# Two-layer masked attention on 16 graphs: other steps for four pieces of batch 14's work, two counts in halves, another buffer and an earlier inversion at the end

## The chip, the cores and the metric

The kernel runs on one core of a Trainium2 chip. The metric is the device time of one execution in microseconds (us); lower is better. The kernel before was run three times: 3083.88 us in the median, from 3083.51 to 3085.02.

## What is computed

The reference takes `x` (16 x 1024 x 256, float32) and a 0/1 adjacency `adj` (16 x 1024 x 1024, int32) and applies two layers of attention with a residual. Cut to what matters:

```python
h = jnp.maximum(_layernorm(x), 0.0)
x = x + L0(h, adj)      # 4 heads of 64
h = jnp.maximum(_layernorm(x), 0.0)
x = x + L1(h, adj)      # 8 heads of 32, with biases on q, k, v
...
# in a layer, for each batch and head:
scores = where(adj > 0, q @ k.T / sqrt(D), -inf)
out = concat_heads(softmax(scores) @ v) @ Wo.T + bo
```

All of it is float32. The softmax is computed as exp(score) over the sum of the exps, without a maximum; a test at the end (`chk`) tells whether a sum left its bounds.

## The kernel before, in words

**Batches and layers.** There are 16 batches (b = 0 to 15). The list of work is layer 0 of batch b + 1, then layer 1 of batch b, and so on, so layer 0 of one batch stands beside layer 1 of another. The last 32 steps are layer 1 of batch 15 alone.

**Groups and steps.** A layer of a batch is cut into two halves of 512 queries (`qh`) and two groups of heads (`g`), so four groups, written (qh, g). A group of layer 1 has 8 steps of 128 keys (j = 0 to 7). For a step i of layer 1, TensorE (PE) makes the scores of four heads (L539, eight matmul instructions into two PSUM pairs), VectorE (DVE) applies the mask and moves them to SBUF (L562, two instructions, one for each pair), and ScalarE (ACT) takes the exp (L568, two instructions). Two steps later (`LEAD`) PE multiplies the exps with v (`weigh`, L580). After an odd step GpSimd (POOL) adds that step's two tiles `p` onto those of the even step before it (L695, two instructions). Tiles of odd steps live in two buffers, so DVE can write step i + 4 only when POOL has added step i. Tiles of even steps live in seven buffers (tag `p0`), so step i + 14 takes the buffer of step i.

**Sums.** The added tiles of a group are added again in memory by a DMA that POOL issues (L681, `accumulate`, 1 MB each). Then `count` (L425) has PE multiply the result with ones, into the PSUM tile `pz`; `halves` does the same in two calls of 256 columns at two steps. From `pz` comes the reciprocal of the sums in five moves, each with its own step: `spread` (L445 copies `pz` on ACT, L458 sends it through four small DMAs into 128 lanes), `invert` (L466 on DVE, then L468, a DMA to DRAM called `vd`), `fetch` (L477, four DMAs that spread `vd` over the partitions as `inv`), `normalize` (L485 on POOL, one multiplication of `cat` for each group of heads), and, for the second group of a half, `end_half`: the product with Wo on PE (L521, sixteen matmuls, the tile `py`) and its addition to x on DVE (L526). The last group of all (`hurry`) uses `finish` instead: it takes the reciprocal on DVE straight from PSUM (L505), multiplies (L506), makes the product in quarters (L496), adds it (L511) and sends it out (L514).

**Units.** The inputs of a layer are made half by half: `stats` (L198 and L199 on DVE for each of four tiles of 256 columns, then four small operations on POOL, L209 to L212, for all four tiles at once), `norm` (L221 on ACT, one for each tile), `turn_blocks` (L273 on DVE), `put_blocks` (L278) and `place_blocks` (L285), which go through DRAM, then the units `k`, `q`, `values` on PE (L307, L383), each emptied by ACT or DVE. `add_bias` is L230 on POOL.

**Order.** The order is written out by hand. `later(i, f)` hangs a piece of work on step i; steps are numbered through. At a step the program issues the scores, then `weigh` of two steps before and the POOL additions, then the counts due, then mask and exp, then the other work due in the order in which it was hung up, and last the units named in `LARGE` (k, q, values, end_half). At an even step with such a unit, `weigh` is put off to the next step. Each engine takes its instructions strictly in this order, and so do the DMA queues of SP and POOL.

**Names used below.** `c` is the first step of layer 1 of batch 14 (`second[14]`, step 704); c + 5 is five steps later. At these steps layer 1 of batch 14 runs, the inputs of layer 1 of batch 15 are made, and the last half of layer 0 of batch 15 is finished: its last group ends at step c - 1 and its `end_group` counts from c + 1. In the diff, `gr.inp.b == B - 1` with layer 0 is this half, `gr.inp.b == B - 2` is layer 1 of batch 14, and `gr.pairs` is layer 1 of batch 15. The groups (0,0), (0,1), (1,0) of batch 14 call `end_group` at c + 9, c + 17 and c + 25. Group (1,0) of batch 15 calls it at step 761; the last scores are those of step 767.

Of the kernel before, what the change touches and what calls it, by code (L numbers as in the profile page):

```python
# [10 lines left out]
F32 = mybir.dt.float32  # L11
# [7 lines left out]
P = 128  # L19
# [71 lines left out]
def fast_program(ctx, tc, a, w, loads, chk):  # L91
# [5 lines left out]
    B, N, E = x.shape  # L97
# [6 lines left out]
    work = ctx.enter_context(tc.tile_pool(name="work", bufs=2))  # L104
# [11 lines left out]
    def psum_pair(name):  # L116
        return ps_s.tile([P, 2, 512], F32, tag="ps_s", name=name)
# [12 lines left out]
    def tiled(cols):  # L130

        return cols.rearrange("p (t g q) -> p t g q", g=4, q=32)
# [260 lines left out]
    class Group:  # L393
# [93 lines left out]
        def finish(self):  # L487

            inp, qh = self.inp, self.qh
            inv = work.tile([P, 512], F32, tag="inv", name=f"inv_{self.n}")  # L490
            py = psum_pair(f"py_{self.n}").rearrange("p a (t e) -> p (a t) e", e=E)
            rows, cat = xs[inp.b, qh], self.half.cat
            dst = quarters(out, inp.b, qh)

            def product(i, c):
                nc.tensor.matmul(  # L496
                    py[:, i, :], cat[:, c, ts(i, P)], w.o[self.layer][:, c, :],
                    start=c == 0 and i % 2 == 0, stop=c == 1 and i % 2 == 1,
                )

            for i in range(4):
                product(i, 0)
            for h in range(2):
                q = ts(h, 256)
                nc.vector.reciprocal(tiled(inv)[:, ts(h, 2)], by_tile(self.s)[:, ts(h, 2)])  # L505
                nc.vector.tensor_mul(cat[:, self.g, q], cat[:, self.g, q], inv[:, q])  # L506
                for i in (2 * h, 2 * h + 1):
                    product(i, 1)
            for h in range(2):
                t = ts(h, 2)  # L510
                nc.vector.tensor_add(rows[:, t, :], py[:, t, :], rows[:, t, :])  # L511
                for g in range(4):
                    queue = nc.scalar if g % 2 else nc.sync
                    queue.dma_start(dst[g][:, t, :], rows[ts(g, 32), t, :])  # L514
# [91 lines left out]
    class Stream:  # L606
# [12 lines left out]
        def later(self, i, f, *args):  # L619
            self.due.setdefault(i, []).append((f, args))  # L620
# [62 lines left out]
        def count_steps(self, i, st):  # L683


            gr, j = st.gr, st.j
            if gr.hurry and j >= NT - 2:
                if st.last:
                    self.counted(i, gr)
                gr.count([of[:, r, :] for of in st.halves for r in range(2)], False, st.last)  # L690
            elif j % 2:
                one = self.steps[i - LEAD - 1].p
                for k, of in enumerate(st.halves):
                    half = one[:, ts(k, 2), :]
                    nc.gpsimd.tensor_add(half, half, of)  # L695
                if gr.pairs and (st.last or gr.hurry):
                    self.later(i + 2, gr.count, one, j == 1, st.last)
                elif gr.pairs:
                    self.halves(i + 3, gr, one, j == 1, False)
                elif j == 1:  # L700
                    gr.one = one
                elif gr.brief:
                    if j == 3:
                        self.accumulate(one, gr.one)
                        self.later(i + 6, gr.count, one, True, False)
                    elif j == 5:
                        self.halves(i + 5, gr, one, False, False)
                    else:
                        self.later(i + 4, gr.count, one, False, True)
                elif j == 5:  # L710
                    gr.two = one
                elif st.last and gr.qh and not gr.g:
                    self.accumulate(one, gr.two)
                    for k, of in enumerate((gr.one, one)):
                        self.later(i + gr.waits, gr.count, of, not k, k == 1)
                elif st.last and gr.last:
                    self.accumulate(gr.two, gr.one)
                    self.later(i + 1, self.accumulate, one, gr.two)
                    self.later(i + gr.waits, gr.count, one, True, True)
                elif st.last:  # L720
                    self.accumulate(gr.two, gr.one)
                    self.later(i + 2, self.accumulate, one, gr.two)
                    if gr.g:
                        self.halves(i + gr.waits, gr, one, True, True)
                    else:
                        self.later(i + gr.waits, gr.count, one, True, True)
                else:
                    self.accumulate(one, gr.one)
                    gr.one = one
# [12 lines left out]
        def end_group(self, i, gr):  # L742

            if gr.hurry:
                for f in (gr.spread, gr.finish, gr.inp.test):
                    self.later(i, f)
                return

            if gr.layer == 0:
                if gr.g == 0:  # L750
                    gr.half.first = gr
                    return
                early = gr.inp.b == 0 and gr.qh
                self.later(i + (2 if early else 3), gr.count_added)
                at = (3, 4, 5, 7, 13) if gr.qh else (3, 5, 6, 7, 11)
                if gr.inp.b == B - 1 and gr.qh:
                    at = 3, 6, 7, 9, 13
                if gr.inp.b == 0:
                    at = (2, 3, 4, 5, 8) if gr.qh else (3, 5, 6, 7, 9)
            else:  # L760
                at = ((9, 11, 13, 19), (8, 12, 14, 17, 19), (7, 9, 11, 14), None)[2 * gr.qh + gr.g]
                if gr.pairs:
                    at = 2, 5, 6, 7, 9
                elif gr.last:
                    at = 4, 6, 7, 9, 11
            for k, f in zip(at, (gr.spread, gr.invert, gr.fetch, gr.normalize)):
                self.later(i + k, f)
            if gr.last:

                k = 7 if gr.layer or gr.inp.b == 0 else 25 if gr.inp.b == B - 1 else 37  # L770
                self.later(i + k, gr.inp.test)
            if gr.g == 1:
                self.later(i + at[4], gr.end_half)
# [80 lines left out]
    later = stream.later  # L854

    def norms(inp, half, *at, whole=False, bias=None):

        for k, i in enumerate(at):
            f, rest = (inp.norm, (whole,)) if k > 1 else (inp.stats, ())
            later(i, f, half, (2, 3) if k % 2 else (0, 1), *rest)  # L860
        later(at[3] + 1 if bias is None else bias, inp.add_bias, half)
# [6 lines left out]
    def block_inputs(inp, half, turn, put, place, *at):  # L868

        later(turn, inp.turn_blocks, half)  # L870
        later(put, inp.put_blocks, half)
        later(place, inp.place_blocks, half)
        parts = inp.k_part, inp.q_part, inp.values_part
        for i, f, part in zip(at, (inp.k, inp.q, inp.values), parts):
            if type(i) is tuple:
                for m in range(2):
                    later(i[m], part, half, m)
            else:
                later(i, f, half)
# [9 lines left out]
    for t in range(NT):  # L889
        i = 7 + 2 * t  # L890
# [8 lines left out]
    for b in range(B - 1):  # L899
        mine, a, c = inputs[1][b], first[b + 1], second[b]  # L900
        if b == 0:

            norms(mine, 0, a + 4, a + 6, a + 7, a + 8, whole=True)
            half_inputs(mine, 0, a + 10, a + 12, a + 13, a + 14)
            norms(mine, 1, a + 10, a + 11, a + 12, a + 13, whole=True)
            half_inputs(mine, 1, a + 15, c, c + 6, c + 2)
        else:
            norms(mine, 0, a - 27, a - 26, a - 19, a - 17, bias=a)
            block_inputs(mine, 0, a - 14, a - 11, a - 5, a, a + 2, a + 8)
            norms(mine, 1, a - 14, a - 14, a - 8, a - 6, bias=a + 6)  # L910
            block_inputs(mine, 1, a, a + 6, a + 7, c, c + (6 if b + 2 < B else 10), c + 2)
        for i, u in zip((0, 2, 4, 6, 7, 9, 11, 13), range(NT)):
            later(a + i, masks[b].second, u)
        if b + 2 < B:
# [13 lines left out]
            at = 5, 8, 10, 12, 14, 45, 49, 51, 53  # L928
# [3 lines left out]
                later(a + at[t + 1] + (1 if t == 4 else 2), mask.flip, t)  # L932
        else:
            last, e = inputs[1][b + 1], c + 32
            later(c + 5, last.stats, 0)
            later(c + 10, last.norm, 0)
            later(c + 13, last.add_bias, 0)
            block_inputs(last, 0, c + 11, c + 12, c + 13, c + 18, c + 22, c + 26)
            later(c + 18, last.stats, 1)
            later(c + 22, last.norm, 1)  # L940
            later(c + 23, last.add_bias, 1)
# [252 lines left out]
```

## Time and profile before

| what | value |
| --- | --- |
| median of three runs | 3083.88 us |
| time of the profiled execution | 3083.88 us |
| its span, first to last instruction | 3082.1 us |
| PE busy | 3061.3 us, 99% of the span |
| DVE, ACT, POOL busy | 80%, 73%, 80% |
| share of PE on the chain that ended last | 92% |
| scores of step c | at 2847.24 us |
| scores of step c + 5 | at 2869.97 us |
| unit k of step c + 18 | at 2913.32 us |
| unit k of step c + 32 | at 2958.86 us |
| scores of the last step (767) | at 3058.69 us |

The page is read from the span down: it gives busy time for each engine, then groups of instructions by line. Since PE is busy nearly everywhere, a mean says little. The timeline of a stretch, which gives the start, the length, the engine, the line and in brackets the idle time before the instruction with what ended it, says where PE took longer than its work needs. Times from here on are us from the start of the span.

### The profile page before, as it was taken

To read this page: it belongs to the slowest core of one execution; us is meant where nothing else is said; L and a number is where in the kernel's file an instruction comes from. 1 tells how busy PE (TensorE), PEld (TensorE's weight loads), DVE (VectorE), ACT (ScalarE), POOL (GpSimd) and SP (SyncE) were. 2 spreads that over 40 slices of the span, in tenths; PEclk is the share of its full clock that TensorE was granted. 3 is DMA by queue.
4 is the path that set the end of the run, shared out by engine and by line. 5 is a ranking of instruction groups with operands and counts; after the bars stand their busy time and mean duration, and the time that the engine had idled before them with its cause. 6 is when DMAs were issued, how large, how long until landed. Compare 5 with 4: busy or idle time off the path is not lost.

```text
span 3082.1 us, 46012 instructions
## 1 busy us (share of the span) xinstructions
PE 3061.3 (99%) x16678; PEld 1199.8 (39%) x16678; DVE 2464.4 (80%) x2712; ACT 2242.9 (73%) x2478; POOL 2462.1 (80%) x1584
## 2 busy tenths in 40 slices
PE   9999999999999999999999999999999999999998
PEld 4443433434334343343433334343343433434333
DVE  6778787887878878787887878878788787887877
ACT  5668777777777767777777777777777777776775
POOL 3578788787887878878788887888878778787886
PEclk9999999999999999999999999999999999999999
DMA  4226556464563645546456463654636546463431
GB/s 134 63 61 147 129 123 135 121 141 121 129 145 110 139 130 133 136 110 138 124 129 138 120 139 108 147 123 122 141 104 144 132 122 138 118 143 86 100 82 34
DMA packets 263548, 372.77 MB, mean 121 GB/s; under 512 B 58768, under 2 KB 218768, under 8 KB 242448
## 3 DMA queue, kind: packets, MB, share of 16 engines
q0 software_dynamic: 23472, 170.93, 28.2%
q1 hardware_dynamic: 239520, 198.56, 22.2%
q8 instruction: 133, 2.18, 0.3%
q14 instruction: 103, 0.84, 0.1%
q10 hardware_dynamic: 320, 0.26, 0.0%
HBM read 149.95 MB, written 47.96 MB: 64 GB/s over the span
## 4 chain that ended last, share of the span: by engine, by line
PE 92%; DVE 2%; DMA 2%; POOL 1%; issue 1%; SPq 1%; ACT 1%; DVEq 0%; ACTq 0%; POOLq 0%
PE ps L539 31%; PE po L580 28%; PE pq L307 10%; PE py L521 7%; PE pv L383 6%; PE pq L348 5%; PE pz L425 4%; PE pv L367 2%; DVE p L562 1%; DMA p<-p 1%; POOL p L695 1%; DMA sums<-s 0%; DMA inv<-vd 0%; ACT p L568 0%; SPq L458 0%
## 5 line engine op out<-in xcount | busy, mean ns | idle before, releaser
L562 DVE SCALAR_TENSOR_TENSOR p<-mask,ps 128x1024 f32<-128x1024 fp8e5 x1536 | 1791.6, 1215 | 346.0 <-PE ps L539 327.2
L568 ACT ACTIVATE p<-p 128x1024 f32<-128x1024 f32 x1536 | 1615.9, 1056 | 597.1 <-DVE p L562 535.4
L695 POOL TENSOR_TENSOR p<-p,p 128x1024 f32<-128x1024 f32 x510 | 1218.1, 2472 | 104.9 <-PE po L580 104.3
L539 PE MATMUL ps<-qT,kT 32*128 32x512 f32 (+1 forms) x6144 | 1089.9, 629 | 5.5 <-DVE p L562 3.5
L580 PE MATMUL po<-p,v 128*32 128x512 f32 (+1 forms) x6144 | 967.9, 599 | 0.4 <-ACT cat L437 0.4
L539 PEld LDWEIGHTS ps<-qT,kT 32*128 32x128 f32 (+1 forms) x6144 | 355.4, 184 | 640.2 <-DVE p L562 269.5
L580 PEld LDWEIGHTS po<-p,v 128*32 128x32 f32 (+1 forms) x6144 | 239.4, 118 | 669.7 <-issue 498.6
L593 POOL TENSOR_TENSOR p<-p 128x1024 f32<-128x1024 f32 x128 | 302.8, 2366 | 79.4 <-DVE p L592 74.1
L592 POOL TENSOR_TENSOR p<-p,p 128x1024 f32<-128x1024 f32 x64 | 151.2, 2363 | 157.3 <-DVE p L589 128.9
L485 POOL TENSOR_TENSOR cat<-cat,inv 128x512 f32<-128x512 f32 x127 | 175.2, 1383 | 77.7 <-DMA inv<-vd 76.5
L521 PE MATMUL py<-wo,cat 128*128 128x256 f32 x1008 | 234.4, 386 | 0.0
L521 PEld LDWEIGHTS py<-wo,cat 128*128 128x128 f32 x1008 | 186.3, 190 | 73.5 <-issue 16.7
L681 POOL DMA_DIRECT2D p<-p x163 | 144.8, 889 | 86.5 <-DMA p<-p 55.2
L383 PE MATMUL pv<-wv,hT 128*128 128x256 f32 x800 | 185.7, 385 | 0.0
L307 PE MATMUL pq<-hT,wq 128*128 128x512 f32 x400 | 184.8, 605 | 0.1
L167 ACT ACTIVATE mask<-adj,numbers 128x1024 fp8e5<-128x1024 int32 x128 | 145.9, 1140 | 45.0 <-DMA adj<-in_adj_dram 45.0
L383 PEld LDWEIGHTS pv<-wv,hT 128*128 128x128 f32 x800 | 148.0, 190 | 57.1 <-issue 25.2
L589 DVE TENSOR_TENSOR p<-p 128x1024 f32<-128x1024 f32 x128 | 166.9, 1304 | 0.0
L526 DVE TENSOR_TENSOR x<-py,x 128x1024 f32<-128x1024 f32 x63 | 77.1, 1224 | 109.1 <-PE py L521 109.1
L437 ACT COPY cat<-po 128x512 f32<-128x512 f32 x128 | 73.7, 576 | 118.5 <-PE py L521 96.6
L595 POOL TENSOR_TENSOR p<-p,p 128x1024 f32<-128x1024 f32 x64 | 151.9, 2373 | 5.0
L230 POOL TENSOR_TENSOR x<-x,bo 128x1024 f32<-128x1024 f32 x64 | 155.7, 2503 | 0.0
(71 smaller groups left out, 1961.2 us busy)
## 6 DMA issues: line engine op xcount, KB each, us to landing
p<-p POOLq DMA_DIRECT2D x163, 1024.0 KB, 7.9
adj<-in_adj_dram SPq DMA_DIRECT2D x512, 128.0 KB, 3.0
turned<-hn SPq DMA_DIRECT2D x58, 512.0 KB, 3.6
hT<-turned SPq DMA_DIRECT2D x232, 128.0 KB, 2.9
x<-in_x_dram SPq DMA_DIRECT2D x128, 128.0 KB, 3.0
inv<-vd SPq DMA_DIRECT2D x128, 128.0 KB, 3.0
inv<-vd SPq DMA_DIRECT2D x252, 64.0 KB, 2.5
out_dram<-x SPq DMA_DIRECT2D x124, 128.0 KB, 2.2
```

The lines of the kernel that those rows point to most:

```text
L230: nc.gpsimd.tensor_add(rows, rows, w.bo[self.layer].unsqueeze(1).to_broadcast([P, 4, E]))
L307: nc.tensor.matmul(pq[:, m, :], wt[self.layer][:, c, ts(m, P)], self.hT[half][:, c, :], start=(c == 0), stop=(c == 1),)
L383: nc.tensor.matmul(pv[:, i, :], self.hT[half][:, c, ts(i, P)], w.v[self.layer][:, c, :], start=(c == 0), stop=(c == 1),)
L485: nc.gpsimd.tensor_mul(o, o, inv)
L521: nc.tensor.matmul(py[:, i, :], self.half.cat[:, c, ts(i, P)], w.o[self.layer][:, c, :], start=(c == 0), stop=(c == 1),)
L539: nc.tensor.matmul(st.ps[i // 2][:, i % 2, :], gr.inp.kT[r * D : (r + 1) * D, gr.g, ts(kt, P)], gr.inp.qT[gr.qh][r * D : (r + 1) * D, gr.g ...
L562: nc.vector.scalar_tensor_tensor(out=half, in0=gr.mask.m[gr.qh][:, kt // 4, :, kt % 4].unsqueeze(1).to_broadcast([P, 2, 512]), scalar=-EDG ...
L568: nc.scalar.activation(half, half, AF.Exp, scale=gr.scale)
L580: nc.tensor.matmul(gr.o[r * D : (r + 1) * D, :], gr.inp.v[:, kt, h * D : (h + 1) * D], st.halves[i // 2][:, i % 2, :], start=(kt == 0), st ...
L589: nc.vector.tensor_add(a, a, b)
L593: nc.gpsimd.tensor_add(a, a, b)
L695: nc.gpsimd.tensor_add(half, half, of)
```

## The change

It has five parts.

1. Layer 0 of batch 15, last half: `invert`, `fetch`, `normalize` and `end_half` one to four steps sooner (c + 6, c + 7, c + 8, c + 10 instead of c + 7, c + 8, c + 10, c + 14); `spread` stays at c + 4.
2. The unit `q` of batch 14's second half goes from c + 10 to c + 6.
3. The statistics for half 0 of batch 15's layer 1 are made in two pieces, tiles 0 and 1 at c + 6 and tiles 2 and 3 at c + 10, instead of all four at c + 5. `norm` goes from c + 10 to c + 10 and c + 12, `add_bias` from c + 13 to c + 14, turn, put and place from c + 11, c + 12, c + 13 to c + 13, c + 14, c + 15. The unit `k` that needs them stays at c + 18.
4. In batch 14, the count of group (0,0) is made in halves at c + 19 and c + 20 instead of whole at c + 18, its `spread`, `invert` and `fetch` two steps later; and the first of the two counts of group (1,0) in halves at c + 28 and c + 29 instead of whole at c + 31.
5. At the end, group (1,0) of batch 15 inverts, fetches and normalizes one step sooner (765, 766, 767 instead of 766, 767, 768), and the reciprocals of `finish` are written into the buffer of tag `hn` instead of one of the two of tag `inv`.

```diff
         def finish(self):
...
-            inv = work.tile([P, 512], F32, tag="inv", name=f"inv_{self.n}")
+            inv = work.tile([P, 4 * E], F32, tag="hn", bufs=1, name=f"inv_{self.n}")[:, :512]
...
                 elif st.last and gr.qh and not gr.g:
                     self.accumulate(one, gr.two)
-                    for k, of in enumerate((gr.one, one)):
-                        self.later(i + gr.waits, gr.count, of, not k, k == 1)
+                    if gr.inp.b == B - 2:
+                        self.halves(i + 3, gr, gr.one, True, False)
+                    else:
+                        self.later(i + gr.waits, gr.count, gr.one, True, False)
+                    self.later(i + gr.waits, gr.count, one, False, True)
...
                     if gr.g:
                         self.halves(i + gr.waits, gr, one, True, True)
+                    elif gr.inp.b == B - 2:
+                        self.halves(i + gr.waits + 1, gr, one, True, True)
...
                 if gr.inp.b == B - 1 and gr.qh:
-                    at = 3, 6, 7, 9, 13
+                    at = 3, 5, 6, 7, 9
...
                 if gr.pairs:
-                    at = 2, 5, 6, 7, 9
+                    at = (2, 4, 5, 6, 9) if gr.qh else (2, 5, 6, 7, 9)
                 elif gr.last:
                     at = 4, 6, 7, 9, 11
+                elif gr.inp.b == B - 2 and not gr.qh and not gr.g:
+                    at = 11, 13, 15, 19
...
-            block_inputs(mine, 1, a, a + 6, a + 7, c, c + (6 if b + 2 < B else 10), c + 2)
+            block_inputs(mine, 1, a, a + 6, a + 7, c, c + 6, c + 2)
...
-            later(c + 5, last.stats, 0)
-            later(c + 10, last.norm, 0)
-            later(c + 13, last.add_bias, 0)
-            block_inputs(last, 0, c + 11, c + 12, c + 13, c + 18, c + 22, c + 26)
+            norms(last, 0, c + 6, c + 10, c + 10, c + 12, bias=c + 14)
+            block_inputs(last, 0, c + 13, c + 14, c + 15, c + 18, c + 22, c + 26)
```

## The prediction

> **What bounds the kernel now.** I read the busy lines, then what PE waited for, then the timelines of the two places that the change touches.
>
> ```profile
> PE 3061.3 (99%) x16678; PEld 1199.8 (39%) x16678; DVE 2464.4 (80%) x2712; ACT 2242.9 (73%) x2478; POOL 2462.1 (80%) x1584
> ...
> PE ps L539 <- DVE p L562: 3.5, 5, 1.2
> PE py L496 <- POOL cat L485: 1.5, 1, 1.5
> ```
>
> PE is the bound almost everywhere, and its idle time is 20.8 us in all (3082.1 - 3061.3), so a change that takes no work off PE can win little. A busy PE can hide waiting, though: eight score matmuls take 1.07 us when nothing holds them and 1.44 to 3.42 us where they wait inside. Comparing each group of matmuls with its own short form, PE loses about 1 us in 48 us up to 2832, and 13 us between 2870 and 2960. That is layer 1 of batch 14, steps c + 5 to c + 32, where no next layer fills PE. The stretch begins so:
>
> ```profile
> 2871.21 2.35 DVE L562 SCALAR_TENSOR_TENSOR p<-mask,ps 128x1024 f32<-128x1024 fp8e5 x2
> 2873.48 0.42 DVE L198 BATCH_NORM_STATS2 st<-x 128x6 f32<-128x256 f32 x1
> ...
> 2876.07 4.58 DVE L562 SCALAR_TENSOR_TENSOR p<-mask,ps 128x1024 f32<-128x1024 fp8e5 x4
> 2877.23 0.89 POOL L681 DMA_DIRECT2D p<-p  x1 [0.30 <-POOL p L695]
> ...
> 2877.32 1.13 PE L539 MATMUL ps<-qT,kT 32*128 32x512 f32 x4 [1.23 <-DVE p L562]
> 2878.37 1.92 PE L580 MATMUL po<-p,v 128*32 128x512 f32 x8
> 2880.85 0.35 SPq L468 DMA_DIRECT2D vd<-vn  x1
> 2886.32 2.40 SPq L477 DMA_DIRECT2D inv<-vd  x4
> ...
> 2890.48 2.51 POOL L485 TENSOR_TENSOR cat<-cat,inv 128x512 f32<-128x512 f32 x2 [0.56 <-DMA inv<-vd]
> 2906.45 9.64 POOL L695 TENSOR_TENSOR p<-p,p 128x1024 f32<-128x1024 f32 x4
> 2911.49 3.48 DVE L562 SCALAR_TENSOR_TENSOR p<-mask,ps 128x1024 f32<-128x1024 fp8e5 x3 [0.27 <-POOL p L695]
> ```
>
> The four statistics hold DVE from 2873.48 to 2876.07 (2.6 us); PE's second pair of scores waits for it until 2877.32. The table of windows gives 0.68 as the granted clock from 2877 to 2881, so `weigh` takes 1.92 instead of 1.06. Then POOL: from 2872.24 to 2916.09 it is busy for 42.61 of 43.85 us, and at 2911.49 (step c + 17) DVE waits for a POOL addition. **Two engines are at their limit in this stretch, DVE and POOL.** The third fact is `vd`: 5.4 us from issue (2880.85) to landing (2886.26), where the same DMA issued at 2846.07 took 1.4; the packets show why, none of it moves until the 1 MB accumulate issued at 2877.23 is through (2878.68 to 2883.57).
>
> The end:
>
> ```profile
> 3058.90 4.73 POOL L695 TENSOR_TENSOR p<-p,p 128x1024 f32<-128x1024 f32 x2 [0.19 <-PE po L580]
> ...
> 3066.68 1.26 POOL L485 TENSOR_TENSOR cat<-cat,inv 128x512 f32<-128x512 f32 x1 [3.05 <-DMA inv<-vd]
> 3067.98 1.76 DVE L505 RECIPROCAL inv<-pz 128x256 f32<-128x256 f32 x1 [5.47 <-POOL cat L485]
> 3072.88 0.19 DVE L953 TENSOR_REDUCE row<-chk 128x1 f32<-128x32 f32 x1 [0.55 <-POOL chk L336]
> 3073.55 1.29 DVE L511 TENSOR_TENSOR x<-py,x 128x512 f32<-128x512 f32 x2 [0.48 <-PE py L496]
> ```
>
> The last reciprocal waits for a multiplication that still reads the buffer it will write, and that waits for a DMA.
>
> **Term 1, steps c + 5 to c + 18 (parts 1 to 3): +3.4 us.** On DVE the move is good: two tiles (1.3 us) each go beside a PE unit of 3.63, under which DVE idles 1.4 to 1.5 us (1.53 at 2890.60). Removed are 2.6 us of DVE, PE's wait and the slow clock. What is late next is POOL and `inv`. With q behind the scores of c + 6 (2873.96 + 3.63 + 1.07 + 1.2), POOL's additions of c + 7 run from 2879.9 to 2884.6, nearly as now (2884.42). Next in its queue now stand the multiplications of L485, at c + 8, ahead of the additions of c + 9 (today behind them).
>
> When does `inv` land? DVE: scores ready 2874.07, mask 2.26, two statistics 1.24, reciprocal 0.25, so `vd` is issued at about 2877.85, 0.62 us after the accumulate. Its packets start 0.84 after issue (3060.34 to 3061.19), those of an accumulate 1.45 after (2877.23 to 2878.68): 2878.69 against 2878.68, a tie. The rows on both sides: a `vd` issued 0.39 after its accumulate landed in 1.4 us (2924.27), a `sums` 0.79 after it first in 5.0 us (2916.56). I take "behind", since it must win on each DMA engine to be ahead: `vd` lands at 2884.2, fetch to both pairs landed 4.0 and 4.9 us (2886.32 to 2890.33 and 2891.21), L485 from 2888.2 to 2890.8. PE, at step c + 10 ready for the product at 2886.4, waits for it 4.4 us: a new wait in place of the old.
>
> The Trainium skill, "DMA: Bandwidth & Descriptors", section "Queues, rings and completion order", says that an engine changes between queues only after a whole packet, some 9 to 17 descriptors; an accumulate has about 8 on each engine here. By that rule a tie lost by any margin costs the whole burst; by the row of 0.39 alone, nothing.
>
> POOL from there, by today's rows (pair of additions 4.7, with an accumulate beside it 5.0; issue 0.9 + 0.3; small operations for the statistics 1.65; bias 2.4): additions c + 9 to 2895.5, issue 2896.7, statistics 2898.2 (today free, in a wait at 2877.9), additions c + 11 to 2902.9, second accumulate after the first landed (2895.8 + 7.3) 2904.0, additions c + 13 to 2908.7, issue 2909.8, bias 2912.0, additions c + 15 to 2914.3 and 2916.7 (today 2911.45). DVE's first mask of c + 17 waits for 2914.3; 1.25 later the scores of c + 18 get their second pair, 1.07 more and k starts at 2916.7, against 2913.32. The turn, two steps later behind a `norm` that waits for POOL's statistics on ACT (2898.2, with the exps of c + 11 behind it), puts hT at about 2916.4 to 2918, no longer 5.3 us ahead of k (2908.02). Ends: with `vd` ahead and no POOL idle left k starts at 2911.5 (-1.8); with `vd` at 2886.26 as today, hT 1.3 late and a slow clock after PE's wait, +6.8.
>
> The skill's "TensorE: Matmul & The Clock Gate", Part 1, has the clock fall after an idle window of about 3.4 us. Here 1.23 us of idle at 2876.1 was followed by the half clock from 2878.44 to 2881.85; by the page the wait of 4.4 us alone would cost some 1.7 us, by the row the old one did too.
>
> **Term 2, the count of (0,0): +0.5 us.** Its 0.99 us ahead of k is in term 1. The tile counted is that of step c + 6, whose buffer step c + 20 takes. So DVE at c + 20 must wait for the second half: scores 1.07, `weigh` 0.88, count 0.43, 0.1, or 2.5 us behind the start of the scores instead of 1.17; the reciprocal and its wait (0.25 + 0.59 at 2923.99) leave the step. +1.33 - 0.84. From -0.8 (all hidden) to +1.3 (the later `sums` also meet an accumulate).
>
> **Term 3, the first count of (1,0): -0.9 us.** Sixteen count matmuls at 2955.96 take 1.83, eight 0.97; 0.86 leaves the step before k, and PE is dense behind it. The halves (0.43 to 0.55) fall on steps c + 28 and c + 29, where scores already take 1.44 because DVE sets the pace. From -0.9 to 0 (DVE waits 1.13 for POOL at 2957.43 anyway).
>
> **Term 4, the end: -0.5 us.** The inversion goes behind DVE's masks of step 765, ending 3057.05 (sums landed 3055.77); `vd` lands 3058.7, `inv` by 3063, so L485 follows the additions at 3063.6. The reciprocal waits only for the count (3065.6). Two times 1.75 with 0.42 each: 3070.0 instead of 3072.32, so 2.3 us sooner. But L953 stands ahead of L511 on DVE and waits for POOL's test, whose sums leave at 3067.60 as before: L511 can start at 3073.07, not 3073.55. I take -0.5 by that row; -1.9 if the order turns (L955 then waits for L953 alone), 0 as the upper end.
>
> Other moves cost nothing: q's buffers are long free at c + 6, put and place pass nothing on SP's queue that is due, and `hn` has had no user since c + 24.
>
> **Sum:** 3.4 + 0.5 - 0.9 - 0.5 = +2.5; on the profiled execution, 3083.88 (span 3082.1 and 1.8 around it, equal to the median of the three): **3086.4 us.**
>
> **Rivals.** (A) `vd` gets ahead: L485 at about 2885, POOL's additions of c + 15 end 1.9 us later than today, k starts at 2913.3, term 1 is 0: -0.9, 3083.0. For it: the tie. Against: one late DMA engine is enough. (B) The cover holds and POOL isn't the limit: term 1 at -1.8, term 2 at -0.8, terms 3 and 4 at -0.9 and -1.9: -5.4, 3078.5; with all of PE's loss up to c + 18 gone, below 3077.7. Against: 42.61 of 43.85. (C) Slower past 0.2%: hT and L485 both behind accumulates: +6.8, +1.3, 0, 0: 3092; it decides if `vd` lands after 2886 and the put meets an accumulate. (D) The early product doesn't wait and nothing shifts: the end alone, 3083.4.
>
> **Chances.** Forecast (3084 to 3089) 46%, A and D 30%, B 12%, half of it below 3077.7, C 12%. A measurement of this kernel can tell about 0.2% (6.2 us) from no change. Faster than that 6%, within it 81%, slower 13% (C and the edge of the forecast). For 8 in 10 the range leaves out the far half of B and most of C: 3080.5 to 3090.2.
>
> **What would show it.** Right: PE idle ahead of the product at c + 10 released by POOL L485; POOL without a gap from there to c + 17; DVE at c + 17 and c + 20 released by POOL and PE; L505 at about 3065.7. Wrong: `vd` landing in 1.4 us, the product starting at 2886, or k of c + 18 before 2912.

## The result, and the profile after

The changed kernel takes 3094.98 us in the median of seven runs (3093.45 to 3095.22), the kernel before 3083.51 in seven beside it (3081.95 to 3085.02). The ratio is 1.0037, with a 95% interval of 1.0025 to 1.0048: slower, by 11.5 us, where 2.5 were forecast. The profiled execution took 3093.45 us, with a span of 3091.7 against 3082.1; it is the fastest of the seven and lies 1.5 us under their median, so the traces account for 9.6 us and the medians for 11.5.

The first block is the page's busy line of the changed kernel; the second is what PE waited for between 2868 and 2968 us (the reader's columns: us in total, times, longest).

```profile
PE 3064.4 (99%) x16694; PEld 1202.8 (39%) x16694; DVE 2458.5 (80%) x2712; ACT 2242.9 (73%) x2478; POOL 2464.7 (80%) x1584
```

```profile
PE py L521 <- POOL cat L485: 4.5, 2, 4.0
PE pq L307 <- DMA hT<-turned: 2.8, 1, 2.8
PE ps L539 <- DVE p L562: 1.3, 2, 0.8
PE ps L539 <- DVE qT L322: 0.5, 1, 0.5
```

Work has hardly changed; sixteen more, shorter matmuls came from the halved counts. Two waits are new: 4.5 us of the product (L521) for POOL's multiplication, and 2.8 of `k` (L307) for `hT`. Busy PE time is 3.1 us higher as well; some of the matmuls ran at half clock. The timeline of the changed kernel shows the first wait:

```profile
2876.49 0.89 POOL L681 DMA_DIRECT2D p<-p  x1 [0.30 <-POOL p L695]
2877.17 0.35 SPq L468 DMA_DIRECT2D vd<-vn  x1
2879.13 4.71 POOL L695 TENSOR_TENSOR p<-p,p 128x1024 f32<-128x1024 f32 x2 [1.75 <-PE po L580]
2884.63 2.40 SPq L477 DMA_DIRECT2D inv<-vd  x4
2888.31 2.49 POOL L485 TENSOR_TENSOR cat<-cat,inv 128x512 f32<-128x512 f32 x2 [4.47 <-DMA inv<-vd]
2889.63 0.70 PE L521 MATMUL py<-wo,cat 128*128 128x256 f32 x2 [4.03 <-POOL cat L485]
2890.76 2.35 POOL L695 TENSOR_TENSOR p<-p,p 128x1024 f32<-128x1024 f32 x1
```

`vd` is issued 0.68 us behind the accumulate and lands at 2884.57, when the accumulate's burst (2877.95 to 2883.57) is through. It did not wait for the whole burst: its 144 packets went out some sixteen at a time, about every 0.63 us, between those of the accumulate (the first at 2878.55, the last at 2883.57). Only when `vd` has landed can `inv` be fetched. POOL, which in the kernel before is busy for 42.61 of 43.85 us here, stands at L485 for 4.47 us with the additions of c + 9 queued behind it, and PE for 4.03. The same profile, from c + 13 to c + 18:

```profile
2903.20 4.99 POOL L695 TENSOR_TENSOR p<-p,p 128x1024 f32<-128x1024 f32 x2
2904.83 1.25 DVE L273 STREAM_TRANSPOSE hn<-hn 128x1024 f32<-128x1024 f32 x1 [0.51 <-ACT hn L221]
2906.11 0.33 SPq L278 DMA_DIRECT2D turned<-hn  x1
2908.49 0.88 POOL L681 DMA_DIRECT2D p<-p  x1 [0.30 <-POOL p L695]
2911.36 4.23 SPq L285 DMA_DIRECT2D hT<-turned  x4
2914.15 1.22 DVE L562 SCALAR_TENSOR_TENSOR p<-mask,ps 128x1024 f32<-128x1024 fp8e5 x1 [1.31 <-POOL p L695]
2916.45 3.48 DVE L562 SCALAR_TENSOR_TENSOR p<-mask,ps 128x1024 f32<-128x1024 fp8e5 x3 [1.08 <-POOL p L695]
2919.31 6.36 PE L307 MATMUL pq<-hT,wk 128*128 128x512 f32 x8 [2.75 <-DMA hT<-turned]
```

The put is issued in the burst of one accumulate (2904.01 to 2909.09) and lands at 2911.29; the place is issued in that of the next (2910.27 to 2916.83), and `hT` lands at 2919.11. In the kernel before the place had one burst ahead of it (2899.04 to 2905.28), `hT` landed at 2908.02 and `k` took 3.70 us without waiting for it. The same two lines, with the count (L425) that then stood ahead of `k`:

```profile
2898.10 4.34 SPq L285 DMA_DIRECT2D hT<-turned  x4
2912.32 1.06 PE L425 MATMUL pz<-p,ones 128*32 128x512 f32 x8
2913.32 3.70 PE L307 MATMUL pq<-hT,wk 128*128 128x512 f32 x8
```

In the changed kernel `k` waits 2.75 us and takes 6.36. The table of windows tells why; its columns are the stretch, its length, busy time of PE, PEld, DVE, ACT and POOL, the granted clock, and the DMA engines:

```profile
2914.49:2917.90 3.41, 1.58 (x8) 0.30 (x4) 2.33 (x3) 1.72 (x3) 3.41 (x2) 1.00 0.93 193
2917.90:2921.32 3.42, 2.01 (x3) 1.01 (x4) 3.28 (x7) 2.98 (x3) 3.42 (x3) 0.50 0.02 4
2921.32:2924.73 3.41, 3.41 (x6) 1.34 (x5) 1.10 (x4) 0.00 (x0) 2.11 (x5) 0.50 0.74 154
```

A stretch in which PE works 1.58 of 3.41 us is followed by two at half clock, and most of `k` (2919.31 to 2925.67) lies in them. The mean granted clock fits: 0.996 to 0.998 in the seven runs of the changed kernel, 0.998 to 0.999 in those of the kernel before.

**Where the time went.** Executions of programs that are alike up to step c + 4 reach it anywhere from 2861.4 to 2864.9 us, so each difference below is taken from the scores of c + 4 in the same execution. In us against the profile of the kernel before, at the start of a step's scores; the ratio is against the runs of the kernel before beside it:

| kernel | c + 10 | c + 18 | c + 19 | c + 26 | c + 33 | c + 63 | median | ratio, interval |
| --- | --- | --- | --- | --- | --- | --- | --- | --- |
| changed | -0.50 | +3.51 | +9.40 | +11.28 | +10.21 | +10.10 | 3094.98 | 1.0037 (1.0025 to 1.0048) |
| E1 late product | -0.50 | +0.17 | +3.89 | +5.74 | +4.67 | +4.57 | 3088.21 | 1.0017 (1.0008 to 1.0026) |
| E2 old statistics | +0.34 | +2.72 | +6.88 | +9.25 | +8.17 | +8.07 | 3092.23 | 1.0034 (1.0021 to 1.0048) |
| E3 whole counts | -0.51 | +3.47 | +6.63 | +5.95 | +5.97 | +5.87 | 3090.22 | 1.0024 (1.0014 to 1.0033) |
| E4 early inversion | -0.51 | -0.96 | +4.41 | +7.74 | +6.75 | +6.94 | 3088.57 | 1.0019 (1.0010 to 1.0029) |
| E5 early block | +0.27 | -1.02 | +3.41 | +6.29 | +5.31 | +5.22 | 3088.01 | 1.0016 (1.0006 to 1.0025) |
| E6 and whole (0,0) | +0.26 | -1.14 | +1.59 | +2.11 | +1.96 | +1.91 | 3086.03 | 1.0009 (1.0000 to 1.0018) |
| E7 before, new end | -1.52 | -1.07 | -0.86 | -0.29 | -0.27 | -0.37 | 3083.05 | 1.0000 (0.9991 to 1.0009) |
| E8 before, (1,0) halves | -1.53 | -1.08 | -0.87 | -0.30 | -0.47 | +0.67 | 3084.41 | 1.0005 (0.9996 to 1.0014) |
| E9 E6, bias late | +0.27 | -1.10 | -0.66 | +0.12 | -0.04 | -0.15 | 3085.14 | 1.0005 (0.9996 to 1.0014) |
| E10 before, biases late | -0.06 | -0.06 | -0.06 | -0.74 | -1.32 | -0.77 | 3081.24 | 0.9994 (0.9985 to 1.0003) |
| E11 E9, both biases late | +0.28 | -1.16 | -0.70 | +1.75 | +0.67 | +0.87 | 3082.52 | 0.9998 (0.9989 to 1.0007) |
| E12 E10, (1,0) halves | -1.52 | -1.09 | -1.10 | -1.78 | -2.85 | -2.05 | 3082.57 | 0.9999 (0.9990 to 1.0008) |

The kernel before had medians of 3082.5 to 3082.8 beside the experiments (25, 33 and 33 runs). The changed kernel's loss is complete at c + 26: 9.4 of 11.3 us arise at two places, `py` at c + 10 and `k` at c + 18, and the other 1.9 between c + 19 and c + 26. E7 and E8 leave c + 5 to c + 26 as it was and still differ from the profile of before by up to 1.5 us there, so a difference of that size in one execution proves nothing by itself; the last section says where part of it comes from.

### The profile page after: what moved, and what is told of

Its sections match the earlier page's. It is cut to its first block, busy times and chain, and to the rows that moved or that the text cites. A ratio compares the mean times of both kernels' runs of the same rounds, so it can differ in the third digit from the quotient of the medians.

```text
span 3091.7 us, 46042 instructions
## 1 busy us (share of the span) xinstructions
PE 3064.4 (99%) x16694; PEld 1202.8 (39%) x16694; DVE 2458.5 (80%) x2712; ACT 2242.9 (73%) x2478; POOL 2464.7 (80%) x1584
## 3 DMA queue, kind: packets, MB, share of 16 engines
q8 instruction: 133, 2.18, 0.3%
## 4 chain that ended last, share of the span: by engine, by line
PE 90%; DMA 3%; DVE 2%; POOL 2%; issue 1%; ACT 1%; SPq 1%; DVEq 0%; ACTq 0%; POOLq 0%
PE ps L539 31%; PE po L580 28%; PE pq L307 9%; PE py L521 7%; PE pv L383 6%; PE pq L348 5%; PE pz L425 4%; PE pv L367 2%; POOL p L695 1%; DVE p L562 1%; DMA p<-p 1%; DMA vd<-vn 1%; DMA inv<-vd 1%; DMA sums<-s 1%; ACT p L568 0%
## 5 line engine op out<-in xcount | busy, mean ns | idle before, releaser
L485 POOL TENSOR_TENSOR cat<-cat,inv 128x512 f32<-128x512 f32 x127 | 176.4, 1394 | 82.1 <-DMA inv<-vd 81.4
L521 PE MATMUL py<-wo,cat 128*128 128x256 f32 x1008 | 236.2, 387 | 4.6 <-POOL cat L485 4.5
L521 PEld LDWEIGHTS py<-wo,cat 128*128 128x128 f32 x1008 | 187.3, 191 | 79.0 <-issue 15.8
L307 PE MATMUL pq<-hT,wq 128*128 128x512 f32 x400 | 184.8, 605 | 0.1
```

What stands on the lines that cost most here:

```text
L307: nc.tensor.matmul(pq[:, m, :], wt[self.layer][:, c, ts(m, P)], self.hT[half][:, c, :], start=(c == 0), stop=(c == 1),)
L485: nc.gpsimd.tensor_mul(o, o, inv)
L521: nc.tensor.matmul(py[:, i, :], self.half.cat[:, c, ts(i, P)], w.o[self.layer][:, c, :], start=(c == 0), stop=(c == 1),)
```

## The experiments

Theory T: the loss comes from two chains of DMAs that the change put behind 1 MB accumulates, `vd` to `py` and put to `k`, and from the clock behind PE's waits. Rival C: the halved counts. Rival P: POOL has no time left in this stretch, so that a wait taken away at one place returns at another.

**E1, part 1 undone.**

```diff
-                    at = 3, 5, 6, 7, 9
+                    at = 3, 6, 7, 9, 13
```

> The changed kernel with part 1 undone: invert, fetch, normalize and product of layer 0 of batch 15 at c + 7, c + 8, c + 10, c + 14 as before. Theory T (the loss comes from two chains of DMAs that stand behind 1 MB accumulates: vd, inv and L485 ahead of the product at c + 10, and put, place and hT ahead of k at c + 18): PE's wait of 4.03 us for L485 goes, with POOL's idle 4.47 us at 2883.8, and c + 11 starts 5 to 6 us sooner; the chain of hT shifts as a whole, so that k still waits 2 to 3 us for it. Time 3088 to 3090. Rival C (the counts in halves and their late sums are most of the loss): 3093 to 3095. Rival P (POOL is full whatever the order of L485, so the wait returns at c + 17 as mask on POOL's addition): c + 18 starts no more than 2 us sooner than in the changed kernel, 3092 to 3093.

3088.21 us, as T has it. The product's wait for L485 is gone, c + 18 starts 3.3 us sooner, and `k` still waits 2.81 us for `hT` and takes 5.37. So part 1 costs 5.5 us by the traces at c + 63 (6.8 by the medians), and the second chain is a loss of its own.

**E2, part 3 undone.**

```diff
-            norms(last, 0, c + 6, c + 10, c + 10, c + 12, bias=c + 14)
-            block_inputs(last, 0, c + 13, c + 14, c + 15, c + 18, c + 22, c + 26)
+            later(c + 5, last.stats, 0)
+            later(c + 10, last.norm, 0)
+            later(c + 13, last.add_bias, 0)
+            block_inputs(last, 0, c + 11, c + 12, c + 13, c + 18, c + 22, c + 26)
```

> The changed kernel with part 3 undone: all four statistics at c + 5, norm at c + 10, add_bias at c + 13, turn, put and place at c + 11, c + 12, c + 13. Theory T: the turned block gets out ahead of the accumulate that now starts 2.1 us before it, hT lands before k is ready and k's wait of 2.75 us and its 2.66 us at half clock go; the four statistics cost 1 to 2 us at c + 7, as in the kernel before; the product at c + 10 waits for L485 as long as in the changed kernel or longer (3.5 to 5 us). Time 3090 to 3092. Rival C: 3093 to 3095. Rival S (the statistics at c + 5 cost more than the late hT, so that moving them was right): 3095 or more.

3092.23 us in five runs, at the upper edge of T. `hT` lands at 2914.56, and PE no longer waits for it. But `k` starts only at 2918.29, behind a mask of DVE that had waited for POOL, and takes 5.12 us, most of it at half clock:

```profile
2917.01 3.48 DVE L562 SCALAR_TENSOR_TENSOR p<-mask,ps 128x1024 f32<-128x1024 fp8e5 x3 [1.08 <-POOL p L695]
2918.29 5.12 PE L307 MATMUL pq<-hT,wk 128*128 128x512 f32 x8 [1.17 <-DVE p L562]
```

The wait and the clock had cost 5.4 us; at c + 19 this kernel is 2.5 us ahead of the changed one, 0.8 of that already at c + 18. That speaks for P.

**E3, part 4 undone**, both counts whole:

```diff
-                    if gr.inp.b == B - 2:
-                        self.halves(i + 3, gr, gr.one, True, False)
-                    else:
-                        self.later(i + gr.waits, gr.count, gr.one, True, False)
-                    self.later(i + gr.waits, gr.count, one, False, True)
+                    for k, of in enumerate((gr.one, one)):
+                        self.later(i + gr.waits, gr.count, of, not k, k == 1)
...
-                    elif gr.inp.b == B - 2:
-                        self.halves(i + gr.waits + 1, gr, one, True, True)
...
-                elif gr.inp.b == B - 2 and not gr.qh and not gr.g:
-                    at = 11, 13, 15, 19
```

> The changed kernel with part 4 undone: the counts of (0,0) whole at c + 18 and the first of (1,0) whole at c + 31, with spread, invert and fetch of (0,0) as before. Theory T: the count of (0,0) falls into the wait for hT and costs nothing there, the 1.9 us that c + 19 to c + 26 lost beyond c + 18 are saved, the (1,0) count costs 1 us again: 3092.5 to 3094.5. Rival C: the loss is mostly here, 3086 to 3089.

3090.22 us, between T and C, and neither had it right. PE at c + 18:

```profile
2915.51 1.13 PE L539 MATMUL ps<-qT,kT 32*128 32x512 f32 x4 [0.40 <-DVE p L562]
2916.57 1.06 PE L425 MATMUL pz<-p,ones 128*32 128x512 f32 x8
2919.44 3.67 PE L307 MATMUL pq<-hT,wk 128*128 128x512 f32 x8 [1.81 <-DMA hT<-turned]
```

`k` starts where it does in the changed kernel (2919.44 and 2919.31), since `hT` sets it. But the count fills 1 us of PE's wait, the clock stays up, and `k` takes 3.67 us, not 6.36. That is the 2.8 us at c + 19. T had no such saving by the clock. Up to c + 26 another 2.6 come back: with whole counts the sums of (0,0) are sent sooner. In the changed kernel they go out beside an accumulate (issued at 2934.07, landed at 2940.58; the accumulate's burst begins at 2934.0), the reciprocal stands on DVE and waits, and the evacuation of `q` and the masks are behind it:

```profile
2940.70 0.25 DVE L466 RECIPROCAL vn<-sums 128x16 f32<-128x16 f32 x1 [3.39 <-DMA sums<-s]
2940.87 1.32 DVE L322 TENSOR_SCALAR qT<-pq,bq 128x512 f32<-128x512 f32 x2
2942.24 2.25 PE L539 MATMUL ps<-qT,kT 32*128 32x512 f32 x8 [0.51 <-DVE qT L322]
```

The accumulate alone does not make this wait: the sums met one in the kernel before as well (issued from 2916.56, the last landed at 2923.87), and there the reciprocal waited 0.59 us. What differs is the room. In the kernel before 6.8 us pass from the issue of the first sums until DVE is free for the reciprocal (2923.40), in the changed kernel 3.2 (2934.07 to 2937.31).

**E4, the inversion a step sooner still**, ahead of the accumulate:

```diff
-                    at = 3, 5, 6, 7, 9
+                    at = 3, 4, 5, 7, 9
```

> The changed kernel with invert and fetch of layer 0 of batch 15 one step sooner still (c + 5 and c + 6; normalize c + 8 and the product c + 10 as in the change). The sums landed at 2873.23 and DVE's masks of c + 5 end at 2872.8 in the changed kernel, so vd is issued at about 2873.6, 2.9 us before the accumulate at 2876.49. Theory T: vd lands 1.4 us later, inv before 2884, L485 runs at once behind POOL's additions of c + 7 (2883.9), and the product waits less than 1 us: POOL gains 4.4 us from there, c + 18 starts 4 to 6 us sooner, hT stays behind its accumulate and k still waits for it: 3088 to 3090.5. Rival P (POOL full): c + 18 no more than 2 us sooner, 3092 to 3093. Rival C: 3093 to 3095.

3088.57 us, as T has it. The timeline of E4:

```profile
2872.14 0.35 SPq L468 DMA_DIRECT2D vd<-vn  x1
2873.62 2.41 SPq L477 DMA_DIRECT2D inv<-vd  x4
2875.01 0.89 POOL L681 DMA_DIRECT2D p<-p  x1 [0.30 <-POOL p L695]
2882.33 2.52 POOL L485 TENSOR_TENSOR cat<-cat,inv 128x512 f32<-128x512 f32 x2
2884.22 3.97 PE L521 MATMUL py<-wo,cat 128*128 128x256 f32 x16
2913.40 5.80 PE L307 MATMUL pq<-hT,wk 128*128 128x512 f32 x8 [2.83 <-DMA hT<-turned]
```

`vd` is issued 2.9 us ahead of the accumulate and lands in 1.4 us instead of 7.4. One of the four fetches still met the accumulate, and landed in time for the second multiplication; L485 and the product, at the same steps as in the change, wait for nothing. c + 18 comes 4.5 us sooner: so much is the order of `vd` and its fetch against one accumulate worth there. `k` waits as in the changed kernel (2.83). Not all of the gain lasts: up to c + 26 E4 loses more than the changed kernel does, with one more stretch of half clock (2938.16 to 2941.58), and at c + 63 3.2 us of it are left (6.4 by the medians).

**E5, both chains put right** (E4, with its `invert` ahead of the other work of c + 5, and the statistics and the block sooner):

```diff
+                if gr.layer == 0 and gr.inp.b == B - 1 and gr.qh and f == gr.invert:
+                    self.due[i + k].insert(0, self.due[i + k].pop())
...
-            norms(last, 0, c + 6, c + 10, c + 10, c + 12, bias=c + 14)
-            block_inputs(last, 0, c + 13, c + 14, c + 15, c + 18, c + 22, c + 26)
+            norms(last, 0, c + 5, c + 6, c + 10, c + 10, bias=c + 14)
+            block_inputs(last, 0, c + 11, c + 12, c + 13, c + 18, c + 22, c + 26)
```

> Early inversion as in the run of that name (invert ahead of the other work of c + 5), and the second chain put right too: statistics at c + 5 and c + 6, all norms at c + 10, turn, put and place at c + 11, c + 12, c + 13; the counts stay in halves and the end stays as in the change. Theory T: the statistics reach POOL in its idle time after the accumulate, the put's packets get out between two accumulates, hT lands about 4 us before k, so k's wait (2.83 us with the early inversion alone) and the half clock behind it go, some 5 us less than the early inversion alone (3088.6): 3083 to 3085. Rival P (POOL's additions set the scores of c + 18 in any order, and the wait only changes its name there): 3086 to 3088.

3088.01 us: T falls short, and P is right, if at the upper edge of its range. `hT` lands at 2909.32, 3.8 us ahead of `k`. The timeline of E5 from c + 17:

```profile
2909.51 1.22 DVE L562 SCALAR_TENSOR_TENSOR p<-mask,ps 128x1024 f32<-128x1024 fp8e5 x1 [2.39 <-POOL p L695]
2910.78 1.13 PE L539 MATMUL ps<-qT,kT 32*128 32x512 f32 x4 [1.56 <-DVE p L562]
2913.08 5.40 PE L307 MATMUL pq<-hT,wk 128*128 128x512 f32 x8 [1.18 <-DVE p L562]
```

Now DVE stands 2.39 us before POOL's addition, PE 1.56 and 1.18 before DVE, and `k` is slow again. So hT's wait had hidden another, behind DVE and POOL, as E2 shows too.

**E6, E5 with the count of (0,0) whole** at c + 18:

```diff
-                    elif gr.inp.b == B - 2:
-                        self.halves(i + gr.waits + 1, gr, one, True, True)
...
-                elif gr.inp.b == B - 2 and not gr.qh and not gr.g:
-                    at = 11, 13, 15, 19
```

> As the run with the early block, but the count of (0,0) whole at c + 18 and its spread, invert and fetch as in the kernel before; the first count of (1,0) stays in halves. Tells what the halves of (0,0) cost when k does not wait for hT. If they cost what whole and halved counts differed by behind c + 19 in the changed kernel (1.9 to 2.7 us), this is 3081 to 3082.5; if they cost the 0.5 us of the prediction, it is 3082.5 to 3084.5.

3086.03 us, above what either expected, but 3.3 us below E5 by the trace (+5.22 to +1.91). DVE's wait of 2.39 us for POOL is still there. The count now lies in PE's wait behind it, 1.18 us in E5 and 0.18 here, and `k` takes 3.70:

```profile
2913.76 1.06 PE L425 MATMUL pz<-p,ones 128*32 128x512 f32 x8
2915.00 3.70 PE L307 MATMUL pq<-hT,wk 128*128 128x512 f32 x8 [0.18 <-DVE p L562]
```

So the halves of (0,0) cost 2 to 5 us in this change, where the prediction had 0.5: 3.3 from E5 to E6 and 4.2 from the changed kernel to E3 by the traces at c + 63, 2.0 and 4.8 by the medians.

**E7, the kernel before with the new end alone** (part 5):

```diff
-            inv = work.tile([P, 512], F32, tag="inv", name=f"inv_{self.n}")
+            inv = work.tile([P, 4 * E], F32, tag="hn", bufs=1, name=f"inv_{self.n}")[:, :512]
...
-                    at = 2, 5, 6, 7, 9
+                    at = (2, 4, 5, 6, 9) if gr.qh else (2, 5, 6, 7, 9)
```

> The kernel before with part 5 alone (the last reciprocals in the buffer hn, the inversion a step sooner). By the trace of the changed kernel the reciprocal waits for ACT's copy of the sums, which ends 0.4 us before POOL's multiplication did in the kernel before; PE then idles 1.6 and 0.9 us and its last products take 1.75 instead of 1.13 us. So the span is within 0.4 us of the kernel before, more likely above, the first reciprocal 8.9 us behind the last scores (9.3 before). The prediction's own step: 0.5 us sooner, the reciprocal 6.9 behind the last scores.

3083.05 against 3082.76 us: no difference that these runs can tell. The timeline of E7:

```profile
3062.95 1.30 POOL L485 TENSOR_TENSOR cat<-cat,inv 128x512 f32<-128x512 f32 x1
3066.36 0.59 ACT L445 COPY s<-pz 128x512 f32<-128x512 f32 x1
3066.99 1.76 DVE L505 RECIPROCAL inv<-pz 128x256 f32<-128x256 f32 x1 [5.22 <-ACT s L445]
3071.38 2.08 PE L496 MATMUL py<-wo,cat 128*128 128x256 f32 x4 [0.93 <-DVE cat L506]
3073.50 1.29 DVE L511 TENSOR_TENSOR x<-py,x 128x512 f32<-128x512 f32 x2 [1.09 <-PE py L496]
```

L485 starts 3.1 us sooner against the last scores, as meant. The reciprocal then starts as ACT's copy of the sums ends, 8.94 us behind the last scores instead of 9.29. The last four products take 2.08 us instead of 1.13, at half clock from 3070.79, and with them L511 starts 15.45 us behind the last scores instead of 14.86.

**E8, the kernel before with the first count of (1,0) in halves**, the first piece of E3's diff the other way round.

> The kernel before with the first of the two counts of (1,0) alone in halves at c + 28 and c + 29. Prediction's term 3, as the trace of the changed kernel has it: c + 32 starts 0.9 to 1.1 us sooner and the whole gains as much, 0.03 per cent, near what five rounds can tell. Rival (DVE's wait for POOL at c + 31 keeps the pace): c + 32 starts no sooner.

3084.41 us, ratio 1.0005 (0.9996 to 1.0014): no gain. c + 32 does start 0.87 us sooner, counted from c + 26. But DVE waits for POOL as before (1.12 us at c + 31), so that 0.70 of it is gone at c + 33, and 1.15 more are lost from c + 51 to c + 52, where `vd` took 3.4 us to land instead of 1.4 and POOL waited for `inv`. A load of 16 KB on the queue that fetches instructions ran in that time (3014.22 to 3015.09); the last 9 of the 144 packets of `vd` moved only as it ended (3015.08).

**E9, E6 with `add_bias` of half 0 at c + 36** instead of c + 14, where POOL has time:

```diff
-            norms(last, 0, c + 5, c + 6, c + 10, c + 10, bias=c + 14)
+            norms(last, 0, c + 5, c + 6, c + 10, c + 10, bias=c + 36)
```

> As the run with the early block and the whole count (3086.0), but add_bias of half 0 (2.67 us of POOL at 2906.42 there) goes from c + 14 to c + 36, where POOL idles over 4 us. Tests whether POOL sets the pace once both chains of DMAs are out of the way. Theory P (POOL's queue between c + 5 and c + 17 is the limit that is left): the additions of c + 15 end 2.3 to 2.7 us sooner, DVE's wait of 2.39 us at c + 17 goes, c + 19 starts 2 to 2.5 us sooner: 3083 to 3084.5. If DVE or PE sets the pace instead: 3085.5 to 3086.5.

3085.14 us, between the two expectations. By the trace it is as P has it: c + 19 comes 2.25 us sooner than in E6 and c + 63 2.06. The medians differ by 0.9 only, which lies within their intervals, so they do not decide. The timeline of E9:

```profile
2906.14 4.79 DVE L562 SCALAR_TENSOR_TENSOR p<-mask,ps 128x1024 f32<-128x1024 fp8e5 x4 [1.10 <-POOL p L695]
2910.60 1.51 PE L539 MATMUL ps<-qT,kT 32*128 32x512 f32 x8
2913.32 3.70 PE L307 MATMUL pq<-hT,wk 128*128 128x512 f32 x8 [0.21 <-DVE p L562]
```

DVE's wait of 2.39 us is 1.10 now, and the scores of c + 18 take 1.51 us without a stop.

**E10, E11, E12: both `add_bias` late** (half 0 at c + 36, half 1 at c + 44): in the kernel before, in E6, and in the kernel before with the (1,0) halves.

```diff
-            later(c + 13, last.add_bias, 0)
+            later(c + 36, last.add_bias, 0)
...
-            later(c + 23, last.add_bias, 1)
+            later(c + 44, last.add_bias, 1)
```

> The kernel before with add_bias of half 0 at c + 36 instead of c + 13 and of half 1 at c + 44 instead of c + 23, nothing of the change. POOL is busy there for 42.61 of 43.85 us, but DVE waits for it only 0.27 us at c + 17 and 1.13 us at c + 31. Theory P: 0.3 to 1.4 us sooner, 3081.3 to 3082.5 against 3082.76. Otherwise no change.

> As the run with the late bias of half 0 on the repaired change, and add_bias of half 1 also late (c + 44 instead of c + 23). Theory P: what DVE waited for POOL at c + 31 goes as well, up to 0.9 us less than that run: 3082.5 to 3084. If nothing waits for POOL there, no less than that run.

> The kernel before with both add_bias late and the first count of (1,0) in halves at c + 28 and c + 29. In the run with these halves alone PE lost at c + 51 what it had gained, since an inv came late there (vd landed in 3.0 us where 1.4 are usual, beside a transfer of 16 KB on the queue that loads instructions). Theory: c + 32 starts 0.9 to 1.8 us sooner than in the kernel before and keeps it if that collision does not come back: 3080.5 to 3082. If it comes back: 3082.5 to 3084.

E10 takes 3081.24 us, the lowest median of all: 1.5 us under the kernel before, ratio 0.9994 (0.9985 to 1.0003). The interval takes in no change, so a gain is likely and not certain; in its trace 0.8 us are gained behind c + 4, and 1.1 ahead of it, where the program is the same. E11 takes 3082.52 us, as much as the kernel before. Its fair counterpart is E10, which has the same late biases, and E11 lies 1.3 us above it, within the intervals: with the chains, the count and POOL put right, the rest of the change is worth nothing that these runs can tell. Against E9 its median is 2.6 us lower, but not its trace: from c + 4 on it is 1.0 longer, with a half clock that costs some 2.4 us from c + 22 to c + 23. E12 takes 3082.57 us. In its trace c + 33 is 2.85 us sooner, of which 1.1 stand at c + 18 already, as in E7, which changes nothing there. At c + 51 `vd` took 3.0 us (3.4 in E8, where the expectation of E12 has 3.0), again with a load of instructions beside it, and 0.8 are lost.

Part 2, `q` at c + 6, was not undone by itself; it is still in E6, E9 and E11.

## Why the prediction missed

The direction was forecast, the size was not: +2.5 against +11.5 us. By its terms:

- **Term 1, `vd` to `py`: right, with some luck.** `vd` behind the accumulate, landing at 2884.57 (2884.2 forecast), L485 from 2888.31 to 2890.80 (2888.2 to 2890.8), the product's wait 4.03 us (4.4). E4 shows it by the opposite order. The landing came out so well since two misses cancel: `vd` took 7.40 us for 6.35, and the execution stood some 0.8 us earlier. That a tie lost costs the whole burst came true only in the time: the packets of `vd` moved from 2878.55 on, between those of the accumulate, and were through with the burst. The row it rests on was read short: of the 5.4 us of `vd` in the kernel before, the last 0.9 lay behind the burst, where 9 of its packets waited for a 16 KB load of instructions (2884.19 to 2885.08). And the "tie" could have been read as "behind" from more rows; the last section has them. The chain of POOL's additions from there to c + 17 came as forecast too: c + 18 starts 3.5 us late.
- **Term 1, `hT`: the step that failed.** It put `hT` "at about 2916.4 to 2918", level with `k` at 2916.7, and took no wait. It priced the delay of the put by the steps that it moved, and did not lay it against the accumulates as it had laid `vd`: the put and the place each met one, `hT` landed at 2919.11, and PE waited 2.75 us for it. Counted from c + 4, `k` starts 6.7 us late, where the term had 3.4. A late `hT` stood in the upper end of the term (+6.8), but the forecast did not use it. The term's 2916.7 was early as well: it overlooked that `k` stands behind DVE's mask of the second pair of c + 17. DVE starts it at 2916.45, when POOL lets it; with its 1.22 us that is some 2917.7, by our estimate.
- **The clock: not priced.** "A slow clock after PE's wait" stood in the upper end only. It cost 2.66 us on `k` alone (6.36 for 3.70), and the product ran partly in a further stretch (2890.59 to 2894.01).
- **Term 2: mis-sized, +0.5 for 2 to 5 us.** The count taken from c + 18 was counted as 0.99 us saved. It lay in a wait that `k` has anyway, so nothing was saved, and it had kept the clock (E3, E6). The sums that were sent two steps later had 3.2 us instead of 6.8 before DVE came to their reciprocal. The end "the later `sums` also meet an accumulate", taken as +1.3, came true, but the sums of the kernel before met one too, so the accumulate is not the difference.
- **Term 3: right in place, -1.07 in the changed kernel** (-0.9 forecast); in the kernel before it did not last (E8), for the reason named as its upper end.
- **Term 4: wrong.** "The reciprocal waits only for the count" does not hold; it started as ACT's copy of `pz` ended. From the last scores to the end of the span it is +0.26 us in the changed kernel, not -0.5.

The sum as it came, by steps: +3.5 at c + 18, +5.9 at c + 18 to c + 19 (1.47 the scores of c + 18, which wait for DVE and it for POOL, 2.75 wait, 2.66 clock, less 0.99 for the count), +1.9 up to c + 26, -1.07 at c + 28 to c + 32, +0.26 at the end. From c + 4 on that is 10.4 us; the changed kernel's execution had reached c + 4 some 0.75 us sooner, which leaves the 9.6 between the two profiles. Single steps of one execution are no surer than the 1.5 us by which E7 differs where nothing was changed. The prediction's rival C had nearly this mechanism, "hT and L485 both behind accumulates", and 12%. Its 3092 counted a slow clock and the late sums, but too low: +6.8 and +1.3, where the trace has +9.4 up to c + 19 and +1.9 behind it. Its condition was put too narrowly, too: `vd` landed at 2884.57, before 2886, and the put met its accumulate all the same.

What the forecast had right about the limits, DVE and POOL, explains why putting the chains right did not bring the time back at once: POOL's queue was the next (E5, E9). In the changed kernel it hides behind `hT`: that wait ends at 2919.11, DVE's would have ended at some 2917.7 (the estimate above), and E2 and E5, where `hT` is early, show DVE's wait of 1.17 and 1.18 us in its place.

## What to carry to other kernels

Before a small DMA is moved, lay its issue, and that of every DMA that follows from it, against the bursts of the large ones: here 2.9 us ahead of an accumulate made 1.4 us of a transfer, and 0.7 behind it 7.4; at 0.3 to 0.4 behind it still took 1.4 (E6, and 2924.27 in the kernel before). Work that fills an engine's wait costs nothing there, and it can hold up the clock; ask what lies in the wait before it is taken away. If two things end at nearly the same time, mending one shows the other, so a repair is priced by the second, not by the first.

## What the runs showed of the hardware

**The clock goes by a grid.** The half clock came in pieces of 3.41 us or twice that, but for the last, which runs to the end of the program. In the changed kernel they begin at 2890.59, 2917.90 and 3081.74, which lie 8.00 and 48.0 pieces of 3.413 us apart. So what a wait costs depends on where it falls. PE's wait of 1.23 us at c + 7 of the kernel before was followed by the half clock in its profile (2878.44 to 2881.85) and in E10; in E7, E8 and E12 the same wait at the same step was not, and c + 8 came 0.86 us sooner, counted from c + 7. Some of the 0.9 to 1.5 us by which unchanged steps differ in the table is this.

The Trainium skill, "TensorE: Matmul & The Clock Gate", Part 1, section "What's actually happening", has a free-running window of 3413 ns, and the grid agrees. It names an idle window as what halves the clock, and the section "Why this matters for your kernels" asks for no gaps over some 3 us; here, by this case's windows, 1.58 us of work in 3.41 was followed by the half clock (two gaps, of 0.49 and 1.34 us), and so were 2.18 in the kernel before and 2.79 in E11 (from 2920.69), while 1.78 in E3, 1.84 in the changed kernel (from 2883.76) and 2.18 in E8 (from 2873.03) were not. The measurements decide: shorter gaps are enough, the busy share alone does not tell, and what the threshold is stays open.

**Some tenths of a microsecond decide whether a small DMA meets a burst.** Over the fourteen traces every `vd` that was issued up to 0.40 us behind the last accumulate landed in 1.4 to 2.8 us, and every one issued 0.59 to 1.42 us behind it took 6.6 to 8.5; in the kernel before alone these are 14 and 12 of them (up to 0.39: 1.4 to 2.5; from 1.06: 7.1 to 8.2). The first packet of `vd` moves 0.84 us after the issue and that of an accumulate 1.45, so 0.6 us behind is where the accumulate begins to be first.

**A reciprocal from PSUM began with the end of a copy.** L505 on DVE started 0.03 us after ACT's copy of the same tile `pz`, in the changed kernel and in E7. The program has DVE wait for ACT there; whether it must was not tried.
